# First group's outputs turned between the last graphs' products, with the first layer's tiles in a pool of their own

## The chip, the cores and the metric

One core of one Trainium2 chip runs the whole program in one launch. The metric is device time in microseconds (us) of one execution, lower is better. Times of several runs are compared by their median.

## The reference, cut to what matters

64 graphs of 256 nodes with 256 features go through two layers, both with a layer norm in front and a residual behind.

```python
# layer 0: graph convolution
h = relu(layernorm(x));  x = x + relu(norm(adj + I) @ h @ W.T + b)
# layer 1, on h = relu(layernorm(x)):
c = relu(bn1(conv1x1(h.T)))                  # conv1
x_conv = relu(bn2(conv17(c)) + h.T).T        # convolution of width 17 along the nodes
s = h @ w_se.T + b_se                        # 3 columns
A = exp(-squared_distance(s, s)) * adj
x_nmp = A @ relu(h @ w_msg.T + b_msg)        # message passing
x = x + GRU(input=[x_conv, x_nmp], state=h)  # gates r, z, n with w_ih, w_hh
```

## The kernel before, in words

**Stages.** Graphs come in four groups of 16 (`NG = 16`, `GROUPS = 4`). The first stage is the loop `for n in range(4, B + 5)` (B = 64): a pipeline over all graphs, in which one turn does one step for each of several graphs. Graph n is aggregated (`ag`) and projected (`o`), graph n-2 is turned (`ht`) and makes its messages (`ms`) and `conv1` (`c`), pairs of graphs get their distances (`st`, `di`, then `e` on ScalarE, `aT` on VectorE or GpSimd), and graph n-5 passes its messages (`nm`, evicted by ScalarE as `xnT` and stored to `xnd` in DRAM). For n of 66, 67 and 68 only the tail of this pipeline is left: the distances of graphs 62 and 63, `conv1` of 63, and the messages of graphs 61, 62 and 63. The second stage is the gates, the loop `for q in range(1, GROUPS + 1)`: 16 graphs in each turn.

**The convolution.** It is done group by group with a Fourier transform of 48 points over overlapping windows. For each graph two spectra (`df`) go from `h1l`, a load of what `conv1` stored, into the tile Xf; 24 steps of products (`y`) with the transformed filter follow; an inverse transform, written as a queue of small steps on VectorE, GpSimd and ScalarE, leaves the outputs in Xf and scr. This queue is `paced`: `beat(us)` is called between PE's pieces of work, runs what `after(k, ...)` has put down for k beats later, and issues as much of the queue as `share` allows; `paced.drain()` issues all that is left. The first group's convolution runs inside the first stage. Group q's outputs must then be turned by 64 PE transposes, four to a PSUM bank (16 banks, `yt`), and evicted with bias and relu into `xcT`, in turns by ScalarE and VectorE. `turn_outputs` does this at the head of each gate loop turn, ahead of the spectra of the next group.

**Order.** PE, VectorE, ScalarE, GpSimd and the DMAs put on `sp` are pinned to the program's order (class `Pinned`), so the order in which the kernel's lines run is the order on each engine. DMAs through `nc.sync` go on the same queue of SyncE (SP), at a place that the scheduler finds. The spectra load ahead by three graphs (`H1 = 3`): the load of graph g+3 is issued when the spectra of graph g are done.

**Memory.** The first stage's pools `ps` (5 PSUM banks), `ps_own` (3 banks), `wts`, `io`, `work` and `small` are closed together at the end of the first stage. The pools of the gates are opened behind that: `ps_m` (3 banks), `ps_gate` (5 banks), and `gates`, which holds xcT (32 KB a partition), the gate weights wiT and whT, and T1 to T4. These lie where the closed pools lay, so their first writers wait for the last users of the closed pools: the load of whT and, before the change, the first evictions into xcT wait for the last message product nm(63) and the last store from xnT. T1 to T4 are made from whT and wiT on GpSimd. The four products `first` write a value into the gates' PSUM banks, and ScalarE copies biases over it. The other state of the convolution (Xf, scr, the streams h1l, wf, xs) is in pools on the right side, which stay open.

**Names and lines.** In the profile almost all instructions carry line 102 (the helper that pins them), so tiles tell them apart. L293 is the load h1l, L328 wf, L1125 the store xnd, L1390 and L1391 the loads of whT and wiT, L1420 and L1421 the two halves of hx, L1427 h2l, L1431 x2l.

Of the kernel before, what the change touches and what calls it, by code (L numbers as in the profile page):

```python
# [11 lines left out]
FP = mybir.dt.float32  # L12
AF = mybir.ActivationFunctionType
ALU = mybir.AluOpType
# [14 lines left out]
OUT = 32  # L29
# [156 lines left out]
def gnn_kernel(  # L186
# [10 lines left out]
    B, N, D = x.shape  # L197
    P = 128
    KW = conv2_w.shape[2]
    NB = N // P  # L200
    DC = D // P
    G = 2
    NR = G * NB
# [25 lines left out]
    ident = const.tile([P, P], FP, tag="ident", name="ident")  # L229
# [15 lines left out]
    paced = Paced(pool, vec, act)  # L245

    def after(beats, go):
        due.append([beats, go])
# [274 lines left out]
                residual(k + 2)  # L523
                k += 1

    def turn_outputs(xcT):

        flip = 0
        for n0 in range(0, OUT, 4):
            for oc in range(DC):  # L530
                t = cv.bank(f"yt_{cv.q}_{n0}_{oc}").rearrange("p (i t) -> p i t", i=4)
                for i in range(4):
                    pe.transpose(
                        t[:, i, :], cv.y[n0 + i][:, oc * P : (oc + 1) * P], ident
                    )
                if (n0 // 4 * DC + oc) % 3 == 2:
                    cv.beat(1.3)
                dst, src = xcT[:, oc, :, n0 : n0 + 4], t.rearrange("p i t -> p t i")
                bias = sh[:, DC + oc : DC + oc + 1]
                flip ^= 1  # L540
                if flip:
                    act.activation(dst, src, AF.Relu, bias=bias)
                else:
                    vec.tensor_scalar(dst, src, bias, 0.0, ALU.add, ALU.max)


    with ExitStack() as one:
        ps = one.enter_context(tc.tile_pool(name="ps", bufs=5, space=PSUM))
        ps_own = one.enter_context(tc.tile_pool(name="ps_own", bufs=1, space=PSUM))
        wts = one.enter_context(tc.tile_pool(name="wts", bufs=1))  # L550
        io = one.enter_context(tc.tile_pool(name="io", bufs=2))
        work = one.enter_context(tc.tile_pool(name="work", bufs=2))
        small = one.enter_context(tc.tile_pool(name="small", bufs=3))
        taps_stack = ExitStack()
        taps = taps_stack.enter_context(tc.tile_pool(name="taps", bufs=1))

# [2 lines left out]
        def beat(us):  # L559
            come_due()  # L560
            paced.issue(*(k * us for k in share))
# [321 lines left out]
        def layer0_in(g, rows):  # L883

            xt, _ = st[g]["both"]
            rsd, nmr, dis = st[g]["rsd"], st[g]["nmr0"], st[g]["dis0"]
            if rows[0] == 0:
                hs = work.tile([P, NR, D], FP, tag="hs", name=f"hs_{g}")
                for b in range(G):
                    rb = slice(b * NB, (b + 1) * NB)  # L890
                    st[g + b].update(hs=hs[:, rb, :], dis=dis[:, rb])
            for r in rows:
                act.activation(
                    st[g + r // NB]["hs"][:, r % NB, :], xt[:, r, :], AF.Relu,
                    bias=nmr[:, r : r + 1], scale=rsd[:, r : r + 1],
                )

        def turn_adj(g, at=(1, 2), by=pool):
            s = st[g]
            t = bank(f"at_{g}").rearrange("p (c i) -> p c i", c=NB)  # L900
            for jc in range(NB):
                for ic in range(NB):
                    pe.transpose(
                        t[:, jc, ic * P : (ic + 1) * P], s["at"][:, ic, jc * P : (jc + 1) * P], ident
                    )

            def keep():
                s["adjT"] = work.tile([P, NB, N], FP, tag="adjT", name=f"adjT_{g}", bufs=6)
                act.copy(s["adjT"], t)

            def hat():
                s["adjH"] = work.tile([P, NB, N], FP, tag="adjH", name=f"adjH_{g}")
                by.tensor_tensor(s["adjH"], s["adjT"], eye, ALU.add)
            after(at[0], keep)
            if at[1] is None:
                return hat
            after(at[1], hat)

        def aggregate(g):
            s = st[g]  # L920
            t = bank(f"ag_{g}").rearrange("p (c i) -> p c i", c=DC)
            for fc in range(DC):
                for jc in range(NB):
                    pe.matmul(
                        t[:, fc, :], s["hs"][:, jc, fc * P : (fc + 1) * P], s["adjH"][:, jc, :],
                        start=(jc == 0), stop=(jc == NB - 1),
                    )

            def keep():
                s["aggT"] = work.tile([P, DC, N], FP, tag="aggT", name=f"aggT_{g}")  # L930
                act.copy(s["aggT"], t)
            after(1, keep)

# [314 lines left out]
        def item(filter_too=False):  # L1248
            if filtering and not filter_too:
                return  # L1250
            pace[1] = min(pace[1] + pace[0], 1.0)
            if items and pace[1] > 0.999:
                pace[1] -= 1.0
                items.pop(0)()
# [29 lines left out]
        begin()  # L1284
        for n in range(4, B + 5):
            even, odd = n % G == 0, n % G == 1
            if filtering and not items:
                filtering.clear()
                while due:
                    beat(0.0)  # L1290
                conv_start()
            if n == B - 2:

                share[:] = 0.45, 0.6, 0.33
            elif n == B:
                share[:] = 0.65, 0.75, 0.4
            if even and n + 2 * G < B:
                load(n + 2 * G)
            if n <= B + 1:
                turn_h(n - 2)  # L1300
            beat(0.4)
            item()
            if n < B:
                aggregate(n)
                if odd and n + 1 < B:
                    after(2, lambda n=n: factors(n + 1))
                    for r in range(NR):
                        after((5, 7, 8, 9)[r], lambda r=r, n=n: layer0_in(n + 1, (r,)))
                if even and n < B - G:
                    for r in (0, 2):  # L1310
                        after(1 + r // 2, lambda r=r, n=n: row_moments(n + G, (r, r + 1)))
                if even and n + G < B:
                    after(4, lambda n=n: degrees(n + G))
            beat(1.7)
            item()
            if even and n <= B + 2:
                turn_cols(n - 4)
            beat(0.2)
            if n + 1 < B:
                turn_adj(n + 1)  # L1320
            beat(0.4)
            item()
            if n >= 5:
                pass_messages(n - 5)
            beat(1.7)
            item(True)
            if n <= B + 1:
                messages(n - 2)
            beat(1.7)
            item()  # L1330
            if even and n <= B + 2:
                distance(n - 4)
            beat(0.6)
            item()
            if n < B:
                project(n)
            beat(1.7)
            item(True)
            if n <= B:
                conv1(n - 2)  # L1340
            elif n == B + 2:
                conv1(B - 1)
            beat(1.7)
            item()
            if later:
                for go in later.pop(0):
                    go()
                if not later:
                    while due:
                        beat(0.0)  # L1350
                    prep_stack.close()
                    spec_stack = ExitStack()
                    spec = spec_stack.enter_context(tc.tile_pool(name="spec", bufs=1))
                    tab = spec.tile([P, 3 * UNITS], FP, tag="tab", name="tab")
                    nc.sync.dma_start(tab, nc.inline_tensor(filter_table(), name="tab_c").ap())
                    tp = {k: filter_load(k) for k in range(2)}
                    filtering.append(True)
                    pace[:] = FILTER / 2, -7.0
                    items.extend(
                        lambda k=k, j=j: filter_part(k, j) for k in range(4) for j in range(QC // 8)  # L1360
                    )
        while items:
            item()
        for g in range(H1):
            h1_load(1, g)
        while due:
# [14 lines left out]
    cv.beat = beat  # L1381
    cv.bank = lambda name: ps_m.tile([P, 2 * D], FP, tag="m", name=name)

    def outputs_turned(q):
        return big.tile([P, DC, P, OUT], FP, tag="xcT", name=f"xcT_{q}")

    xcT = outputs_turned(1)
    wiT = big.tile([P, 2 * DC, 3 * D], FP, tag="wiT", name="wiT")
    whT = big.tile([P, DC, 3 * D], FP, tag="whT", name="whT")
    nc.sync.dma_start(whT, wh_d)  # L1390
# [220 lines left out]
    for q in range(1, GROUPS + 1):  # L1611
# [1 line left out]
        ld = gate_inputs(q - 1, 0)  # L1613
        paced.drain()
        if q > 1:
            xcT = outputs_turned(q)
        turn_outputs(xcT)
        for go in gate_parts(ld, xcT):
            go()
        todo = []  # L1620
# [57 lines left out]
```

## Time and profile before

| | us |
|---|---|
| median of 3 runs (2075.66, 2078.24, 2078.29) | 2078.24 |
| the profiled execution | 2076.19 |
| its span, first to last instruction | 2074.4 |
| PE busy in it (98%) | 2029.9 |
| DVE, ACT, POOL busy | 1403.6, 999.2, 1108.7 |
| mean granted PE clock | 0.997 |

A line of a timeline gives the start, the length from the first start to the last end, the engine, the line, the operation with out<-in, the count, and in brackets how long the engine was idle before it and what ended that. The program's fp32 matmuls run as two passes, so `nm` of one graph shows as x8; a transpose is one. SPq lines are the issue of a DMA and not its transfer. A windows line gives for each engine the busy time in that stretch, then the granted clock of PE, the mean share of the DMA engines that was busy, and GB/s.

### The profile page before, as it was taken

The page shows a single profiled execution, that of the slowest core. Times are in us where ns is not written, and L with a number is a line of the kernel's source. Part 1 is how long each engine was busy: PE and PEld are TensorE (multiplying, and loading weights), DVE is VectorE, ACT ScalarE, POOL GpSimd, SP SyncE. Part 2 cuts the span into 40 slices and gives each one's busy share as a digit, 9 for nine tenths or more (in the row PEclk, how much of TensorE's full clock was granted, in tenths as well). Part 3 has the DMA queues.
Part 4 walks back from the last instruction along what each step waited for, and adds up shares of the span by engine and source line. Part 5 has one row for each costly group of instructions (what it writes and reads, how often), then busy time and mean ns, then how long its engine had stood idle before and what let it go on. Part 6 is the DMA issues. An engine that isn't in the chain of part 4 may idle for free. (4 is left out here: it accounts for less than half of the span.)

```text
span 2074.4 us, 31212 instructions
## 1 busy us (share of the span) xinstructions
PE 2029.9 (98%) x9977; PEld 1728.6 (83%) x9977; DVE 1403.6 (68%) x3172; ACT 999.2 (48%) x2171; POOL 1108.7 (53%) x1326
## 2 busy tenths in 40 slices
PE   7999999999999999999999999999999999999998
PEld 6877777888888787788888888888888888888887
DVE  5656666544688888237889815989924989965444
ACT  5756666665457676522344532234442234443333
POOL 4343333334775665347667527766626767644433
PEclk9999999999999999999999999999999999999999
DMA  8797987656765554656333455533446524322331
GB/s 282 261 259 245 265 257 248 208 178 224 240 206 198 178 178 138 212 178 204 122 117 117 137 176 190 168 101 118 124 152 199 155 92 129 116 87 89 95 96 61
DMA packets 292488, 352.84 MB, mean 170 GB/s; under 512 B 19523, under 2 KB 232150, under 8 KB 291670
## 3 DMA queue, kind: packets, MB, share of 16 engines
q1 hardware_dynamic: 292038, 346.40, 53.1%
q0 software_dynamic: 288, 4.46, 0.6%
q8 instruction: 80, 1.31, 0.3%
q14 instruction: 82, 0.67, 0.1%
HBM read 224.43 MB, written 126.35 MB: 169 GB/s over the span
## 5 line engine op out<-in xcount | busy, mean ns | idle before, releaser
L102 DVE TENSOR_TENSOR Xf<-y,k 128x256 f32<-128x256 f32 x184 | 69.0, 416 | 177.8 <-PE y L102 174.8
L102 DVE SCALAR_TENSOR_TENSOR Xf<-Xf 128x256 f32<-128x256 f32 (+1 forms) x248 | 185.1, 760 | 6.2 <-ACT Xf L102 5.1
L102 PE MATMUL ta<-T,S 128*128 128x256 f32 x768 | 186.6, 379 | 0.0
L102 PE MATMUL y<-wf,Xf 128*128 128x256 f32 x768 | 182.5, 380 | 1.8 <-DVE Xf L102 1.4
L102 POOL TENSOR_TENSOR rz<-u,p 128x256 f32<-128x256 f32 x64 | 47.8, 747 | 244.4 <-ACT u L102 244.4
L102 POOL TENSOR_TENSOR rs<-ve,mhalf 128x2 f32<-128x2 f32 x65 | 52.1, 801 | 220.0 <-DVE nm L102 218.7
L102 ACT ACTIVATE rz<-rz 128x512 f32<-128x512 f32 x128 | 80.3, 627 | 180.8 <-DVE rz L102 180.8
L102 PEld LDWEIGHTS y<-wf,Xf 128*128 128x128 f32 x768 | 143.9, 190 | 24.1 <-DVE Xf L102 2.6
L102 PEld LDWEIGHTS ta<-T,S 128*128 128x128 f32 x768 | 145.9, 190 | 19.8
L102 PE MATMUL n<-wiT,hx 128*128 128x256 f32 x512 | 152.3, 379 | 0.0
L102 POOL TENSOR_TENSOR xs<-Xf 128x256 f32<-128x256 f32 x92 | 69.8, 765 | 136.2 <-PE y L102 72.2
L102 DVE SCALAR_TENSOR_TENSOR h2l<-rz,h2l 128x256 f32<-128x256 f32 x128 | 102.9, 804 | 53.4 <-POOL h2l L102 53.4
L102 POOL TENSOR_TENSOR aT<-e,adjT 128x512 f32<-128x512 f32 x62 | 83.1, 1357 | 95.0 <-ACT e L102 95.0
L102 PE MATMUL ms<-wmT,h2T 128*128 128x259 f32 x512 | 127.2, 391 | 4.4 <-ACT h2T L102 4.4
L102 PE MATMUL n<-whT,hx 128*128 128x256 f32 x512 | 131.4, 379 | 0.0
L102 PE MATMUL n<-wiT,xcT 128*128 128x256 f32 x512 | 131.4, 379 | 0.0
L102 PE MATMUL nm<-aT,mso 128*128 128x256 f32 x512 | 123.3, 385 | 6.1 <-DVE pre L102 3.6
L102 PE MATMUL ag<-adjH,hs 128*128 128x256 f32 x512 | 124.3, 385 | 4.8 <-POOL adjH L102 2.7
L102 POOL TENSOR_TENSOR adjH<-adjT,eye 128x512 f32<-128x512 f32 x63 | 82.2, 1305 | 83.0 <-ACT adjT L102 81.2
L102 PE MATMUL o<-w0T,aggT 128*128 128x256 f32 x512 | 124.0, 385 | 1.4 <-ACT e L102 0.9
L102 PEld LDWEIGHTS ms<-wmT,h2T 128*128 128x128 f32 x512 | 97.8, 194 | 32.1 <-issue 12.9
L102 PE MATMUL c<-w1T,h2T 128*128 128x256 f32 x512 | 123.0, 383 | 0.0
(190 smaller groups left out, 5259.4 us busy)
## 6 DMA issues: line engine op xcount, KB each, us to landing
wf<-wfd SPq DMA_DIRECT2D x284, 256.0 KB
wfd<-fo SPq DMA_DIRECT2D x32, 576.0 KB
x2d<-x SPq DMA_DIRECT2D x64, 256.0 KB
h2d<-h SPq DMA_DIRECT2D x64, 256.0 KB
hTd<-h2T SPq DMA_DIRECT2D x64, 256.0 KB
h1d<-c1o SPq DMA_DIRECT2D x64, 256.0 KB
xnd<-xnT SPq DMA_DIRECT2D x64, 256.0 KB
h1l<-h1d SPq DMA_DIRECT2D x64, 256.0 KB
```

The source lines that it names most:

```text
L102: return self.tc.keep_in_program_order(getattr(self.engine, op)(*args, **kwargs))
```

## The change

Three things are done.

- `hs`, `adjH` and `aggT`, tiles of the first layer, move from pool `work` to pool `io`, with the same two buffers. `io` (with x and adj, too) gets a stack of its own, `front_stack`, opened behind `small`.
- At n = B + 2 = 66 `front_stack` is closed, a pool `turned` for xcT is opened on the right side, and the paced queue is drained. xcT of all groups comes from this pool, and no longer from `gates`.
- `turn_outputs` is split: `turn_part_of` writes the four transposes of one bank and hands back its eviction. The first group's 16 banks are placed in the last turns of the first stage: one at n = 66 behind the messages of graph 61, three at the end of n = 66, six at n = 67 ahead of the messages of graph 62, and two times three behind the loop. Each eviction is put down for the next beat. They use the first stage's `bank` (5 PSUM buffers). For groups two to four the same banks are turned at the head of the gate loop, as before.

```diff
-    def turn_outputs(xcT):
-
-        flip = 0
-        for n0 in range(0, OUT, 4):
-            for oc in range(DC):
-                t = cv.bank(f"yt_{cv.q}_{n0}_{oc}").rearrange("p (i t) -> p i t", i=4)
...
+    def outputs_turned():
+        return cv.turned.tile([P, DC, P, OUT], FP, tag="xcT", name=f"xcT_{cv.q + 1}")
+
+    def turn_part_of(xcT, k):
+
+        n0, oc = k // DC * 4, k % DC
+        t = cv.bank(f"yt_{cv.q}_{n0}_{oc}").rearrange("p (i t) -> p i t", i=4)
+        for i in range(4):
+            pe.transpose(t[:, i, :], cv.y[n0 + i][:, oc * P : (oc + 1) * P], ident)
+        dst, src = xcT[:, oc, :, n0 : n0 + 4], t.rearrange("p i t -> p t i")
+        bias = sh[:, DC + oc : DC + oc + 1]
+
+        def keep():
+            if k % 2 == 0:
+                act.activation(dst, src, AF.Relu, bias=bias)
+            else:
+                vec.tensor_scalar(dst, src, bias, 0.0, ALU.add, ALU.max)
+        return keep
+
+    TURNS = OUT // 4 * DC
+
+    def turn_outputs(xcT, ks=range(TURNS)):
+        for k in ks:
+            keep = turn_part_of(xcT, k)
+            if k % 3 == 2:
+                cv.beat(1.3)
+            keep()
...
-        io = one.enter_context(tc.tile_pool(name="io", bufs=2))
         work = one.enter_context(tc.tile_pool(name="work", bufs=2))
         small = one.enter_context(tc.tile_pool(name="small", bufs=3))
+
+        front_stack = ExitStack()
+        io = front_stack.enter_context(tc.tile_pool(name="io", bufs=2))
...
-                hs = work.tile([P, NR, D], FP, tag="hs", name=f"hs_{g}")
+                hs = io.tile([P, NR, D], FP, tag="hs", name=f"hs_{g}")
...
         for n in range(4, B + 5):
             even, odd = n % G == 0, n % G == 1
+            if n == B + 2:
+
+                front_stack.close()
+                cv.turned = ctx.enter_context(tc.tile_pool(name="turned", bufs=1, side="right"))
+                paced.drain()
+                xcT, parts_left = outputs_turned(), list(range(TURNS))
+
+                def turns(m):
+                    for _ in range(m):
+                        after(0, turn_part_of(xcT, parts_left.pop(0)))
...
+            if n == B + 3:
+                turns(6)
+                beat(0.0)
             if n >= 5:
                 pass_messages(n - 5)
             beat(1.7)
+            if n == B + 2:
+                turns(1)
             item(True)
...
             elif n == B + 2:
                 conv1(B - 1)
             beat(1.7)
+            if n == B + 2:
+                turns(3)
+                beat(0.0)
             item()
...
         while items:
             item()
+        for _ in range(2):
+            turns(3)
+            beat(0.0)
         for g in range(H1):
             h1_load(1, g)
...
-    def outputs_turned(q):
-        return big.tile([P, DC, P, OUT], FP, tag="xcT", name=f"xcT_{q}")
-
-    xcT = outputs_turned(1)
...
         if q > 1:
-            xcT = outputs_turned(q)
-        turn_outputs(xcT)
+            xcT = outputs_turned()
+            turn_outputs(xcT)
```

More of the change, by code (lines that the diff above doesn't have):

```diff
@@ L524, in inverse_last @@
                 k += 1
-    def turn_outputs(xcT):
-        flip = 0
-        for n0 in range(0, OUT, 4):
-            for oc in range(DC):
-                t = cv.bank(f"yt_{cv.q}_{n0}_{oc}").rearrange("p (i t) -> p i t", i=4)
[L532 to L544, printed above, removed]
+    def outputs_turned():
[20 more added lines that the diff above has]
+            keep()
     with ExitStack() as one:
@@ L911, in hat @@
             def hat():
-                s["adjH"] = work.tile([P, NB, N], FP, tag="adjH", name=f"adjH_{g}")
+                s["adjH"] = io.tile([P, NB, N], FP, tag="adjH", name=f"adjH_{g}")
                 by.tensor_tensor(s["adjH"], s["adjT"], eye, ALU.add)
@@ L929, in keep @@
             def keep():
-                s["aggT"] = work.tile([P, DC, N], FP, tag="aggT", name=f"aggT_{g}")
+                s["aggT"] = io.tile([P, DC, N], FP, tag="aggT", name=f"aggT_{g}")
                 act.copy(s["aggT"], t)
```

## The prediction

> **What bounds the kernel now.** I read the busy table first: PE is busy for 2029.9 of 2074.4 us (98%), so only time in which PE idles or runs at a lower clock can be won. The chain that ended last shows only the final two DVE instructions and says nothing of the middle. So I cut the span into windows of 20 us: from 840 to 860 us PE is busy for 17.59 us only. That is the seam between the first layer and the gates, the place of the change. There I went through the timelines engine by engine. PE first; the columns are start, length, instruction, and the idle time before it with what ended it.
>
> ```profile
> 834.64 1.89 PE L102 MATMUL nm<-aT,mso 128*128 128x256 f32 x8
> 836.46 0.71 PE L102 MATMUL di<-R,L 5*128 5x256 f32 x8
> 837.11 1.99 PE L102 MATMUL c<-w1T,h2T 128*128 128x256 f32 x8
> 838.93 3.62 PE L102 MATMUL nm<-aT,mso 128*128 128x256 f32 x16
> 843.27 1.14 PE L102 MATMUL first<-brzB,ident 32*128 32x512 f32 x8 [0.72 <-ACT xnT L102]
> ...
> 846.82 1.94 PE L102 MATMUL yt<-ident,Xf 128*128 128x128 f32 x14 [0.94 <-ACT xcT L102]
> ...
> 853.20 5.13 PE L102 MATMUL df<-dft,h1l 128*128 128x240 f32 x24
> 859.07 5.48 PE L102 MATMUL df<-dft,h1l 128*128 128x240 f32 x24 [0.75 <-DMA h1l<-h1d]
> 864.85 16.44 PE L102 MATMUL df<-dft,h1l 128*128 128x240 f32 x80 [0.29 <-DMA h1l<-h1d]
> 881.12 4.02 PE L102 MATMUL y<-wf,Xf 128*128 128x256 f32 x16
> ```
>
> To be seen: after the last message product (end 842.55) come `first`, the 64 transposes `yt` (844.34 to 853.20) and the spectra `df`, and the spectra already wait for loads. Then the same stretch on SP, which issues the DMAs in program order:
>
> ```profile
> 841.52 2.05 SPq L1125 DMA_DIRECT2D xnd<-xnT  x2
> 845.43 0.32 SPq L1390 DMA_DIRECT2D whT<-whd  x1
> 845.80 0.42 SPq L1391 DMA_DIRECT2D wiT<-wid  x1
> 846.27 0.43 SPq L1420 DMA_DIRECT2D hx<-hTd  x1
> 846.74 0.85 SPq L1421 DMA_DIRECT2D hx<-xnd  x1
> ...
> 855.11 0.32 SPq L293 DMA_DIRECT2D h1l<-h1d  x1
> ```
>
> The gates' weights whT (768 KB) and wiT (1536 KB) go out only when the last `xnd` store has landed, 2.88 us after the last message product, and the fourth `h1l` (256 KB) stands behind them. Last, windows of 1 us after a PE gap of 2.53 us (the third number from the right is the granted clock):
>
> ```profile
> 826.00:827.00 1.00, 0.00 (x0) 0.00 (x0) 1.00 (x4) 1.00 (x5) 0.00 (x0) 1.00 0.00 0
> ...
> 829.00:830.00 1.00, 1.00 (x4) 0.82 (x3) 0.90 (x3) 0.75 (x3) 0.58 (x1) 0.50 0.14 38
> 830.00:831.00 1.00, 1.00 (x3) 0.73 (x3) 1.00 (x2) 0.18 (x1) 1.00 (x2) 0.50 0.91 257
> ```
>
> An idle PE comes back at half clock. The four rows from 828 to 832 have 0.68, 0.50, 0.50, 0.61: 1.71 us lost. The gap of 2.1 us at 143 us cost about the same (0.85, 0.50, 0.50, 0.50, 0.95).
>
> **The change, part by part.** It adds and removes no instruction: the built orders show the same instructions, and apart from the seam the same sequence, on all engines (groups two to four turn their outputs as before).
>
> *The pools.* hs, adjH and aggT keep their two buffers, only at another address; before the seam no wait changes. Cost 0; I see no row that would price an address. The paced work of the first group ends on DVE at 833.3 and on POOL at 833.9, ahead of the point where it is now drained: cost 0, bounds 0 to 0.4 us (one 128x256 DVE operation ahead of the column copies).
>
> *The wait that goes.* Before, xcT lies over the closed pools, so its first writes wait for the same `xnd` store as whT (landed by 845.43; DVE's first eviction starts at 845.63, ACT's at 846.09 behind its bias copies), and PE stands 0.94 us. That goes. The other 52 of the 64 transposes then take 6.38 us, 0.49 us a bank of four, with three banks; bare transposes follow each other in 0.11 us, 0.44 a bank. With five banks, and evictions of 0.69 us (ACT) and 0.75 us (DVE) taking turns, the evictions need 0.75 us per two banks, less than PE, and no longer bind. I take 0.46 a bank, bounds 0.44 and 0.53.
>
> *The new order on PE.* One bank after nm(61), nine between c(63) and nm(62), six after nm(63). The ten banks ahead of nm(63) make its end 842.55 + 10 x 0.46 = 847.15. What they wait for is there: aT(62) follows e, which slips by one ACT eviction (0.69) to about 839.2, and nm(62) stands at 843.5. Six banks: 849.9. `first` now has to wait until the last bank is evicted (its latency 0.17, DVE 0.75, a semaphore 0.06: 1.0) : 850.9; `first` takes 1.07 (843.27 to 844.34): the spectra start at 851.95 instead of 853.20. **Gain on PE 1.25 us.** The idle of 2.53 us at 825 and its half clock lie ahead of the seam and stay.
>
> *What is moved with it.* nm(63) ends 4.6 us later, so the last `xnd` store, and whT, wiT, hx behind it on SP, go out 4.6 us later: whT at 850.03. Behind nm(63) on ACT stands only its own copy, so nothing is added there. POOL's T products wait for wiT; they ended at 862 and would end at 866.6, and the first gate needs them at 891: hidden by the spectra. But the fourth `h1l` is late. The new order on SP helps it: hx of the second graph and h2l now stand behind it. Ahead of it remain whT, wiT and two hx, 2.88 MB, with itself 3.15 MB. By the 1 us windows the queue before had moved 3.15 MB at 854.6, 9.2 us after the issue of whT (no bytes in the first 1.3 us). What waits sees its data later than that: T on POOL 0.9 us (wiT, 853.56), S on DVE 2.4 us (hx, 856.36), PE 1.7 us (3.93 MB by 857.3, spectra at 859.07). I take 1.7, the row of the same tile: 850.03 + 9.2 + 1.7 = **860.9**, bounds 860.1 and 861.6 (with 0.53 a bank 862.3). The spectra ask for it at 851.95 + 6 x 0.81 = 856.8. PE stands 4.1 us, where before it stood 1.0 (858.06 to 859.07).
>
> *After the stall.* Before, the remaining 26 spectra took 22.05 us (859.07 to 881.12) where 26 x 0.81 = 21.06 would do; 1.0 us was waiting for the next loads. In the new order the fifth and sixth `h1l` land right behind the fourth, and the seventh (4.72 MB, moved by 15.1 us after whT's issue, 866.8 with the lag) is asked for at 860.9 + 4.86 + 1.7 = 867.5: I take that wait as 0, bound 1.0. The half clock I take at 1.7, bounds 0 and 1.8: the gap is longer than the two gaps that cost that much. So the products start at 860.9 + 21.06 + 1.7 = 883.7 instead of 881.12: **+2.6 us**. From there PE is nearly always busy (1207.6 of 1220 us from 840 to 2060) and nothing later absorbs a shift. 2076.19 + 2.6 = **2078.8 us** (span 2074.4 + 2.6, and the 1.8 us around it). The profiled execution lies 2.05 us under the median shown, 2078.24; against that it would be 2080.8.
>
> *Two rules against it.* The Trainium skill, TensorE: Matmul & The Clock Gate, Part 1, sets the clock down after an idle window of about 3.4 us. The gaps of 2.1 and 2.5 us above contradict that as a limit for one gap; if it held strictly and the stall were just under 3.4, the sum would be +0.9 us. The Trainium skill, DMA: Bandwidth & Descriptors, Specifications, gives 435 GB/s as the ceiling: estimate 3.15 MB in 7.2 us, `h1l` there at about 858.6, a short stall, products at 879.6, 1.5 us earlier than before. The rows have 3.15 MB in 7.9 us and a lag behind it.
>
> **The rivals.**
> - *The load is not late* (it lands as wiT did, or the scheduler's earlier place on SP is worth more than I count). Then 851.95 + 32 x 0.81 = 877.9, 3.2 us early: 2073.0. For it: the first three `h1l` are there long before. Against: DMA is full (0.96 to 1.10) from 847 to 852 already.
> - *Late, but no half clock*: 860.9 + 21.06 = 882.0, +0.9: 2077.1. For it: gaps of 0.7 to 1.1 us had none. Against: three longer gaps had it.
> - *Slower by more than 0.2%*: the load block starves the spectra further. With 0.53 a bank and the lag of hx (2.4), the fourth `h1l` is there at 850.7 + 9.2 + 2.4 = 862.3; with 1.75 of half clock and a second wait of 1.0 at the seventh: 886.1, +5.0: 2081.2. It decides from a start of the fourth graph's spectra at 862.5 on, or 861.5 with the second wait. For it: before, DMA is at 0.74 to 1.10 from 847 to 863, and now 4.6 us later. Against: hx and h2l have moved behind.
> - *It gains more than 0.2%*: the first rival's 3.2 us, 0.3 from 0.44 a bank, and 0.5 if the last bank is evicted in half the time, make 4.0: 2072.2, not even then. It would take something that I do not see.
>
> That the turns do not move is excluded by the built order.
>
> **How the numbers follow.** 0.2% is 4.2 us, about what a measurement of this kernel can tell from no change. Forecast (late, half clock) 0.55; late without half clock 0.15; not late 0.13; further starved 0.14; a gain over 4.2 us 0.03. The first three lie within 0.2%: 0.83. The range runs from the first rival, 2073.5, to the starved case with the 2 us by which runs differ, 2083.0.
>
> **What would show it.** Right: nm(63) ends near 847; whT goes out near 850; PE waits some 4 us for `h1l` after six spectra (24 `df` rows), with clock rows of 0.5 behind; xcT's evictions wait for `yt` alone; products near 883.7. Wrong: spectra without a wait (first rival), no rows of 0.5, a second wait at the seventh graph, or evictions that stop `yt` between the products. Any difference ahead of 834 us would be a cost of the pools that I put at 0.

## The result, and the profile after

The changed kernel takes 2080.6 us (median of 20 runs, 2078.38 to 2084.06), the kernel before 2077.62 us in 20 runs beside it: ratio 1.0018, 95% interval 1.0012 to 1.0024, so 2.98 us slower by the medians. The profiled execution takes 2079.66 us (span 2077.9); predicted were 2078.8 against a profiled 2076.19, and 2080.8 against the median.

The PE timeline of the changed kernel through the seam, in the columns of the prediction's first fence:

```profile
833.86 0.66 PE L102 MATMUL st<-ident,cols 128*128 128x128 f32 x4 [2.74 <-DVE cols L102]
...
843.30 3.62 PE L102 MATMUL nm<-aT,mso 128*128 128x256 f32 x16
846.76 2.13 PE L102 MATMUL yt<-ident,Xf 128*128 128x128 f32 x18
...
850.48 1.14 PE L102 MATMUL first<-brzB,ident 32*128 32x512 f32 x8 [0.93 <-DVE xcT L102]
851.55 5.13 PE L102 MATMUL df<-dft,h1l 128*128 128x240 f32 x24
859.89 10.02 PE L102 MATMUL df<-dft,h1l 128*128 128x240 f32 x40 [3.22 <-DMA h1l<-h1d]
870.65 13.20 PE L102 MATMUL df<-dft,h1l 128*128 128x240 f32 x64 [0.74 <-DMA h1l<-h1d]
883.69 4.02 PE L102 MATMUL y<-wf,Xf 128*128 128x256 f32 x16
```

The transposes now lie ahead of the second `nm` row and behind it; PE goes from them into `first` and the spectra `df`, which start 1.65 us earlier than before (851.55 against 853.20; 0.28 us of that lies ahead of the seam). Then PE stands 3.22 us for the fourth `h1l`, where it stood 0.75 us, and 0.74 us again at the ninth. SP's timeline of the same kernel shows why the load is late:

```profile
845.89 2.04 SPq L1135 DMA_DIRECT2D xnd<-xnT  x2
849.79 0.32 SPq L1417 DMA_DIRECT2D whT<-whd  x1
850.16 0.42 SPq L1418 DMA_DIRECT2D wiT<-wid  x1
...
853.46 3.56 SPq L293 DMA_DIRECT2D h1l<-h1d  x3
```

whT goes out at 849.79 instead of 845.43, since the last `xnd` store comes behind ten more banks of transposes. The fourth `h1l` goes out at 853.46, when the first graph's spectra have freed a buffer, and 6.43 us later PE goes on. The windows of 1 us of PE around the stall (busy share, granted clock, DMA share, GB/s):

```profile
857.00:858.00 1.00, 0.00 (x0) 1.00 0.96 367
858.00:859.00 1.00, 0.00 (x0) 1.00 1.05 406
...
860.00:861.00 1.00, 1.00 (x4) 0.70 0.90 307
861.00:862.00 1.00, 1.00 (x4) 0.50 1.02 387
862.00:863.00 1.00, 1.00 (x4) 0.50 0.70 252
863.00:864.00 1.00, 1.00 (x4) 0.59 0.24 43
```

PE idles while the DMA engines are full, and comes back at half clock: 0.30 + 0.50 + 0.50 + 0.41 = 1.71 us lost. The span grew by 3.5 us: -0.28 ahead of the seam (start of `st`), +2.85 in it (`st` to the first products `y`: 46.98 before, 49.83 now), +0.93 behind it.

### The profile page after: what moved, and what is told of

Same layout as the page of the kernel before. It is cut to its first block, busy times and chain, and to the rows that moved or that the text cites. A ratio compares the mean times of both kernels' runs of the same rounds, so it can differ in the third digit from the quotient of the medians.

```text
span 2077.9 us, 31212 instructions
## 1 busy us (share of the span) xinstructions
PE 2028.0 (98%) x9977; PEld 1727.6 (83%) x9977; DVE 1402.2 (67%) x3172; ACT 998.8 (48%) x2171; POOL 1108.9 (53%) x1326
```

## The experiments

Executions reach the seam at different times, so I compare inside it. In the table, "stall" is PE's wait for the fourth `h1l`, with later ones of the same tile behind a plus, and "half" the time lost to half clock inside the seam. All are from the one profiled execution of each kernel, while the ratio to the kernel before is from the timed runs.

| kernel | st to spectra | stall | half | st to products | ratio (95%) |
|---|---|---|---|---|---|
| before | 19.06 | 0.75 + 0.29 | 0 | 46.98 | 1 |
| changed | 17.69 | 3.22 + 0.74 | 1.7 | 49.83 | 1.0018 (1.0012 to 1.0024) |
| pools_only | 19.05 | 0.67 + 0.16 | 0 | 46.38 | 0.9999 (0.9990 to 1.0008) |
| first_last | 19.66 | 1.08 | 0 | 47.00 | 1.0002 (0.9993 to 1.0010) |
| pools_first_last | 19.69 | 1.57 | 1.5, at `st` | 47.52 | 0.9997 (0.9987 to 1.0006) |
| behind | 17.40 | 1.97 | 1.7 | 47.32 | 1.0001 (0.9992 to 1.0010) |
| behind_wi_twice | 17.40 | 4.98 | 2.0 | 50.85 | 1.0020 (1.0011 to 1.0029) |
| extra | 17.69 | 0 + 0.76 | 0 | 44.72 | 0.9988 (0.9979 to 0.9997) |
| behind_extra | 17.40 | 0 | 0 | 43.43 | 0.9989 (0.9980 to 0.9998) |
| act_queue | 17.69 | 3.23 | 1.6 | 48.78 | 1.0002 (0.9993 to 1.0012) |
| early_wh_pin | 17.69 | 1.63 | 0 | 45.58 | 0.9989 (0.9981 to 0.9998) |
| before_pin2 | 19.05 | 0 | 0 | 45.07 | 0.9995 (0.9986 to 1.0004) |
| behind_pin2 | 17.40 | 0.26 | 0 | 43.92 | 0.9984 (0.9976 to 0.9993) |

**Theory:** the seam is longer because whT and wiT go out later and the spectra's fourth load stands behind them. **Rivals:** the pools' new addresses cost the time (A); the turns between the products cost PE time (C); the DMA's bandwidth binds anyway, so that a stall only moves (D).

### One part at a time: pools_only, behind

pools_only is the changed kernel with the turns put back to the head of the gates:

```diff
-            if n == B + 2:
-                turns(1)
...
         if q > 1:
             xcT = outputs_turned()
-            turn_outputs(xcT)
+        turn_outputs(xcT)
```

> Only the pools and the drain of the change; the turns stand where they stood before, with three PSUM buffers. Theory (the later loads cost the time): the first xcT eviction no longer waits for the last xnd store, so the spectra start 0.9 to 1.1 us earlier than before (852.1 to 852.3 in the profile), but whT goes out as early as before (845 to 846), so the fourth h1l still lands at 858.5 to 859.2: the gain turns into a longer wait of PE for h1l (1.5 to 2.2 us instead of 0.75), the products start at 881 (880.6 to 881.6), or at 882.5 if the clock halves behind that wait; ratio 0.9995 to 1.001. Rival A (the pools' new addresses cost the time): products as late as in the changed kernel, 883 to 884, or a loss ahead of 834 us; ratio 1.0015 to 1.002. Rival B (the removed wait is a gain in full): products at 880, ratio 0.9995.

The ratio and the products are those of the theory (46.38 from `st`, the fourth `h1l` 13.57 us after whT's issue, against 13.64 before), and rival A is out as the cause of the loss: with the new addresses the kernel is no slower than before, to within 0.1%. (Behind the products its traced execution takes 1.27 us longer than that of before, 1194.55 against 1193.28 us; pools_first_last, with the same pools, has 1193.31.) One expectation missed: the spectra did not start earlier. PE waited as long as before the change, though no closed pool lies under xcT any more. The PE row and ACT's rows of pools_only, then ACT's rows of before:

```profile
847.84 1.94 PE L102 MATMUL yt<-ident,Xf 128*128 128x128 f32 x14 [0.95 <-ACT xcT L102]
```

```profile
845.45 0.38 ACT L102 COPY ta<-brzB 128x256 f32<-128x256 f32 x1 [1.21 <-PE first L102]
845.76 0.37 ACT L102 COPY tc<-brzB 128x256 f32<-128x256 f32 x1
846.07 1.10 ACT L102 COPY n<-bnB 128x512 f32<-128x512 f32 x2
847.11 1.26 ACT L102 ACTIVATE xcT<-yt,sh 128x512 f32<-128x512 f32 x2
```

```profile
845.05 1.10 ACT L102 COPY n<-bnB 128x512 f32<-128x512 f32 x2
846.09 1.25 ACT L102 ACTIVATE xcT<-yt,sh 128x512 f32<-128x512 f32 x2
```

In both, ACT's first eviction stands without a gap behind its four bias copies for `first` (ta, tc and two of n). In pools_only these, not the store, end the wait. The next section but one takes that apart.

behind keeps five PSUM buffers and turns all banks behind the last `nm`:

```diff
...
-        for _ in range(2):
-            turns(3)
+        for m in (3, 3, 3, 3, 3, 1):
+            turns(m)
             beat(0.0)
```

> The change with all 16 banks turned behind the last message product, still in five PSUM buffers, none between the products. Theory (the later loads cost the time): the last xnd store and whT go out some 4.4 us earlier than in the changed kernel (whT at 845 to 846), PE has the same work ahead of the spectra, so these start where they start in the changed kernel, 851.3 to 852; the fourth h1l lands at 858.5 to 859.2, so PE waits 1.7 to 2.8 us; products at 881 without, at 882.5 with a stretch of half clock; 1 to 2.7 us less than the changed kernel, ratio to before 0.999 to 1.0007. Rival A (the pools' addresses cost the time): as slow as the changed kernel, ratio 1.0015 to 1.002. Rival C (turns between the products cost PE time of their own, loads do not matter): the spectra start more than 1 us earlier than in the changed kernel, 850.5 or before, and the wait for h1l stays as long as in the changed kernel, 3.2 us.

PE of behind:

```profile
858.46 22.98 PE L102 MATMUL df<-dft,h1l 128*128 128x240 f32 x104 [1.97 <-DMA h1l<-h1d]
```

As the theory has it: whT at 845.24, spectra at 851.36, stall 1.97 us, products at 881.28, 2.51 us less from `st` than the changed kernel. Of these, 1.25 us are the shorter stall, 0.74 the second wait that is gone, 0.29 the earlier spectra, and 0.23 is in none of these rows (a wait in brackets counts from the modelled end of the last matmul and so falls short of the delay of the next start: 0.74 for some 0.9 us at the second wait). The 0.29 us is all that is left of rival C. Against before, the wait that went came back as a stall and half clock: ratio 1.0001.

### The stall alone: extra, behind_extra, early_wh_pin, behind_wi_twice

extra is the changed kernel with the fourth to sixth `h1l` loaded at n = 66 into tiles of their own; behind_extra the same on behind:

```diff
...
+                cv.more = ctx.enter_context(tc.tile_pool(name="more", bufs=1, side="right"))
+                for g in range(H1, 2 * H1):
+                    h1 = cv.more.tile([P, NB, D], FP, tag=f"h1m{g}", name=f"h1m_{g}")
+                    nc.sync.dma_start(h1, h1_d[NG + g].rearrange("p (c d) -> p c d", c=NB))
+                    cv.h1[1, g] = h1
```

> The change as it is, turns between the products, but the fourth to sixth h1l of the second group are loaded ahead of the seam into tiles of their own, so that six graphs of spectra wait for nothing behind whT and wiT. Theory: whT still goes out near 850, the spectra start near 851.6, and PE does not stand at the fourth graph; no rows of half clock there; products at 877.5 to 878.5 (a wait of up to 1 us at the seventh graph is possible), 5 to 6 us less than the changed kernel and 2.7 to 3.6 less than before; ratio to before 0.998 to 0.9988. Rival A or C (addresses, or the order of the turns on PE): the time stays that of the changed kernel, ratio 1.0015 to 1.002, whatever the spectra wait for. Rival D (the stall only moves to later graphs, bandwidth binds): PE waits 2 to 3 us at the seventh graph instead, products at 881 to 883.

> The turns behind the last message product as in the run named behind, and the three extra h1l tiles. Theory: with the loads ahead neither place of the turns starves the spectra, so this one and the run named extra come out alike: spectra at 851.3 to 852, products at 877.5 to 878.5, ratio to before 0.998 to 0.9988, within 0.5 us of each other at the products. Rival C (the place of the turns itself counts): this one is 1 us or more ahead of the run named extra at the products. Rival D (bandwidth binds): a wait of 2 to 3 us at the seventh graph in the run named extra, less here.

PE of extra:

```profile
857.25 5.02 PE L102 MATMUL df<-dft,h1m 128*128 128x240 f32 x24
862.11 5.02 PE L102 MATMUL df<-dft,h1l 128*128 128x240 f32 x24
867.90 11.58 PE L102 MATMUL df<-dft,h1l 128*128 128x240 f32 x56 [0.76 <-DMA h1l<-h1d]
879.32 4.02 PE L102 MATMUL y<-wf,Xf 128*128 128x256 f32 x16
```

With the turns between the products and whT as late as in the change (850.57), taking the stall away takes 5.11 us off the seam: 3.22 of stall, 1.7 of half clock. Rival D shows in small (0.76 us at the tenth graph's load, not 2 to 3). The two kernels differ by 1.29 us at the products in the profile, more than I expected, and that is the mark I had set for rival C. But only 0.29 of it is the spectra's start; 0.76, as counted in the brackets, is that wait for a load. Their ratios cannot be told apart.

early_wh_pin takes whT out of the way (in the new pool, loaded ahead of the seam). Up to the fourth `h1l` the rest of the order is the change's; behind it, all `h1l` go ahead of the loads of later graphs, by the edit described below for before_pin2, so that only its first wait is to be compared:

```diff
+                cv.whT = cv.turned.tile([P, DC, 3 * D], FP, tag="whT", name="whT")
+                nc.sync.dma_start(cv.whT, wh_d)
...
-    nc.sync.dma_start(whT, wh_d)
+    whT = cv.whT
     nc.sync.dma_start(wiT, wi_d)
...
```

> The change as it is, turns between the products, but whT (0.79 MB) has a tile in the new pool and is loaded ahead of the seam; the loads keep the change's order up to the fourth h1l, with 2.36 MB up to and with it instead of 3.15. Theory (the bytes asked for from the seam on set the stall, 0.39 MB per us): 2.0 us less, PE waits 0.9 to 1.6 us for the fourth h1l instead of 3.22, and no half clock follows, since PE does not idle for 1.8 us within one window; from st to the products 45 to 46.5 us instead of 49.83; ratio to before 0.9990 to 0.9999. Rival (the stall is the latency from the issue of the load itself, or what the turns do): the wait stays 3 us, with half clock behind it, 49 us or more, ratio 1.001 to 1.002.

The stall fell by 1.59 us to 1.63, just past the end of what I expected (1.6), and no half clock followed:

```profile
859.16 21.30 PE L102 MATMUL df<-dft,h1l 128*128 128x240 f32 x104 [1.63 <-DMA h1l<-h1d]
```

From the issue of the first of the weights to PE's go on it takes 8.43 us instead of 10.10: 0.79 MB for 1.67 us. behind_wi_twice goes the other way, with wiT loaded twice on behind (no more than a repeated load):

```diff
     nc.sync.dma_start(wiT, wi_d)
+    nc.sync.dma_start(wiT, wi_d)
```

> The run named behind, with wiT loaded twice (the same data into the same tile); the second load and three of hx stand ahead of the fourth h1l: 4.98 MB up to and with it instead of 3.93. Theory (the queue's bytes ahead of the fourth h1l set the stall): 1.05 MB more at 0.39 MB per us is 2.7 us more: PE waits 4.3 to 5.2 us instead of 1.97; from st to the products 50 us (49.3 to 51) instead of 47.32; ratio to before 1.0008 to 1.0020. Rival (the stall is not set by these bytes): the wait stays 2 us, st to the products 47.3, ratio as for behind, 1.000.

Stall 4.98, `st` to products 50.85, ratio 1.0020. The size does not prove the rate, though: the second load had to wait for the first to land (issued at 853.94), and the fourth `h1l` behind it went out only at 854.30.

### What the removed wait was for: first_last, pools_first_last

first_last leaves the pools of before and moves the products `first`, with ACT's copies behind them, from ahead of the transposes to behind them; pools_first_last does that on pools_only.

```diff
-    for r, tag in enumerate(("ta", "tc", "n", "n")):
...
         turn_outputs(xcT)
+        if q == 1:
+            for r, tag in enumerate(("ta", "tc", "n", "n")):
...
```

> The kernel before, its pools and three PSUM buffers unchanged; only the four small products called first (and with them ACT's bias copies, which wait for them) stand behind the 64 transposes instead of ahead of them. It tells what the 0.94 us wait of PE was for. Theory Q (ACT's queue: the bias copies of 1.66 us stood ahead of ACT's first eviction): the first evictions start 0.3 us after the first transposes, at 843 to 844, ahead of the time at which whT goes out (845.2 to 845.8); PE stands less than 0.4 us in a stretch between the transposes; from the start of the last column transposes st to the spectra 18.0 to 18.4 us instead of 19.06. Theory S (my prediction's: xcT lies over closed pools and waits for the last xnd store): no eviction before 845.2; PE stands 1.5 to 2.2 us after three banks; st to spectra 19.6 to 20.2 us. In both the fourth h1l lands where it did, 858.5 to 859.2, so the products start within 0.7 us of before (plus 1.7 if the clock halves); ratio 0.9995 to 1.001.

> Both edits of the runs named pools_only and first_last together: xcT in the pool of its own, and first with ACT's bias copies behind the transposes; turns at the head of the gates as before, three PSUM buffers, loads in the order of pools_only. Theory Q and S together (two waits of nearly one length lay over each other, so that either alone leaves PE standing 0.95 or 1.48 us): no stretch of PE's waiting for xcT is longer than 0.35 us, and from st to the spectra it takes 18.0 to 18.5 us instead of 19.05 and 19.66. Theory B (three PSUM buffers are what holds PE, whatever the evictions wait for): 0.9 us or more of waiting stays, st to the spectra 18.9 or more. The fourth h1l lands at the same time after whT's issue as in pools_only (13.6 us), so st to the products stays within 46 to 47.2 us (1.7 more with half clock); ratio 0.999 to 1.001.

In first_last the store does hold the evictions, as theory S has it. The PE and the ACT row:

```profile
847.01 1.94 PE L102 MATMUL yt<-ident,Xf 128*128 128x128 f32 x14 [1.48 <-ACT xcT L102]
```

```profile
846.27 1.27 ACT L102 ACTIVATE xcT<-yt,sh 128x512 f32<-128x512 f32 x2 [2.32 <-DMA xnd<-xnT]
```

With both edits (pools_first_last) no wait for xcT is left at all; the row in which it stood has no idle time ahead of it:

```profile
845.47 2.50 PE L102 MATMUL yt<-ident,Xf 128*128 128x128 f32 x18
```

From `st` the spectra start after 19.69 us, not 18.0 to 18.5, because this execution ran `st` and the first `nm` behind it at half clock (1.54 us lost ahead of the transposes). Counted from the second-last message product, which starts behind that stretch, the four kernels need 14.27 (before), 14.26 (pools_only), 14.87 (first_last) and 13.36 us (both). So two waits of about the same length lay over each other, and either alone kept PE standing. Three PSUM buffers are not the limit (theory B): the 13.36 us were made with them. Less the 1.54 us, `st` to products is 45.98, at the lower end of what was expected.

### Whose bytes: act_queue

```diff
-        nc.sync.dma_start(h1, h1_d[q * NG + g]
+        (act if q == 1 and g >= H1 else nc.sync).dma_start(h1, h1_d[q * NG + g]
```

> The change as it is, with the thirteen h1l issued on ACT's queue instead of SP's; the same bytes are in flight. It tells whether the fourth h1l is late because it stands behind whT, wiT and hx in one queue, or because the bandwidth is used up. Theory ring: a queue of its own shares the DMA engines with SP's, so the fourth h1l lands 2 us or more earlier after its issue, PE waits 0 to 1.2 us instead of 3.22, no half clock, st to the products 44.7 to 46.5 us instead of 49.83; ratio to before 0.9985 to 0.9998. Theory bandwidth: the bytes asked for first are moved first whatever the queue; PE still waits 2.7 to 3.5 us; st to the products 49 to 50.3; ratio 1.001 to 1.002. ACT has each issue between its copies of the spectra; if they delay these, PE waits for ACT in many small steps.

The fourth `h1l` was issued at 853.21 and let PE go at 859.64, 6.43 us later; in the changed kernel 853.46 and 859.89, 6.43 us too. A queue of its own did not help this load. In the trace's DMA records its packets start at 856.6, 3.4 us after the issue, and from 857 to 861 the two queues move 0.40 MB per us, 0.23 on SP's and 0.17 on ACT's; so neither theory holds as I put it. The second wait went (0.74 us). The ratio, 1.0002, came out lower than the 1.001 I expected; a seam 1.80 us longer than before's would make 1.0009, which lies within its interval.

### The order alone: before_pin2, behind_pin2

Both issue the thirteen `h1l` ahead of hx, h2l and x2l of the later graphs, by putting these loads on SP in program order (`sp.dma_start` in place of `nc.sync.dma_start`); before_pin2 does nothing else to the kernel before.

> The run named behind with the same loads, but issued on SP in the order whT, wiT, two hx of the first graph, and then all thirteen h1l ahead of hx, h2l and x2l of the later graphs. Theory: 3.15 MB up to the fourth h1l instead of 3.93, 2.0 us less: it is there at about 856.4 when the spectra ask for it at 856.2: PE waits 0 to 0.6 us, no half clock there; from st to the products 43.5 to 44.5 us instead of 47.32; ratio to before 0.9983 to 0.9993. Rival D (the bytes are only moved, and hx or wf come too late for the gates): products as early, but PE waits 2 us or more for hx, h2l or wf between 885 and 930, ratio 0.9995 to 1.001. Rival A (something else than the loads makes the seam long): st to the products stays above 46.

> The kernel before with no part of the change, only the loads in the order of the run named behind_pin2 (the thirteen h1l ahead of hx, h2l and x2l of the later graphs). It tells how much of that run's gain is the order of the loads alone. Theory: the spectra start 19.06 us after st as before, the fourth h1l is there before they ask for it, so from st to the products 19.06 + 32 x 0.81 = 45.0 to 45.4 us instead of 46.98: 1.6 to 2.0 us less than before, and 1.1 to 1.5 us more than behind_pin2 (43.92), which is what the earlier spectra of the change are worth once the loads do not hide it; ratio to before 0.9988 to 0.9996. Rival (the order gives all of the gain, the place of the turns nothing): st to the products 43.9, ratio 0.998 to 0.9988. Rival (order alone gives nothing): 46.9, ratio 1.000.

PE of behind_pin2, then of before_pin2 (a row without brackets has no wait ahead of it):

```profile
858.28 21.30 PE L102 MATMUL df<-dft,h1l 128*128 128x240 f32 x104 [0.26 <-DMA h1l<-h1d]
879.41 4.02 PE L102 MATMUL y<-wf,Xf 128*128 128x256 f32 x16
```

```profile
853.09 26.19 PE L102 MATMUL df<-dft,h1l 128*128 128x240 f32 x128
879.11 4.02 PE L102 MATMUL y<-wf,Xf 128*128 128x256 f32 x16
```

Both seams are as the theory has them. The order alone takes 1.91 us off the seam of before (ratio not to be told from 1), and with the loads out of the way the change's earlier spectra are worth another 1.15 us. behind_pin2 has the lowest ratio of the study, though its interval overlaps with those of extra, behind_extra, early_wh_pin and before_pin2: 2074.21 us against 2078.05, ratio 0.9984 (0.9976 to 0.9993). Its last 0.26 us is a wait for the fourth `h1l`: issued at 854.80, when the first graph's spectra free its buffer, it lets PE go on 3.48 us later. This is not the least that the load takes: in before_pin2 it was issued at 855.01 and held nothing up at 858.05, 3.04 us later. There the DMA engines had run nearly dry (49 and 6 GB/s from 854 to 856), while in behind_pin2 they were still moving 354 and 162 GB/s; that these bytes make the difference is likely, but no run shows it.

## Why the prediction was right

- **Bound and place** (PE at 98%, the seam): right. pools_only shows no cost of the pools that its interval of 0.1% could tell. The idle of 2.53 us at 825 stayed; its half clock did not in the traced execution, which won nothing by it, since PE then waited 2.74 us for `cols` at `st` instead of 1.06.
- **The wait that goes: right in size, wrong in cause.** The prediction has the evictions wait for the `xnd` store. The store landed by 845.43, but ACT's first eviction, which held PE, started at 846.09 right behind its bias copies. Its row was before me, and I set the copies down as a remark. The two lay over each other, and by the runs with `first` moved the wait goes only because the change also puts `first` behind the turns.
- **The new order on PE**: gain 1.37 us (19.06 to 17.69), forecast 1.25. A bank took 0.436 us, not 0.46; nm(63) ended at 846.92, forecast 847.15; the wait ahead of `first` was 0.93, forecast 1.0.
- **What is moved with it: right, and the step that decided.** whT at 849.79 (850.03), the fourth `h1l` at 859.89 (860.9), stall 3.22 (4.1). The windows have 3.15 MB moved at 858.9, 9.1 us after whT's issue (9.2). The lag behind the bytes is the term mis-sized: 1.0 us, where the prediction took 1.7 from the row of before. extra, behind and early_wh_pin show that this stall and what follows it is the loss.
- **After the stall**: half clock 1.7, as forecast. The second wait, taken as 0 with a bound of 1.0 at the seventh graph, was 0.74 at the ninth. It offset the shorter stall, so that the products at 883.69, forecast 883.7, agree to a hundredth by luck; from `st` it is 49.83 us against 49.6.
- **"Nothing later absorbs a shift"**: the shift was not absorbed, but 0.93 us came on top behind the products. PE's waits for the filter stream `wf` are 0.9 us there (one of 0.40 at 917.26), and before has none of them; but its waits for `h1l` are 0.3 us shorter, and all its idle time from the first products to the last matmul grew by 0.45 us (9.55 to 10.00), half of the 0.93. Between the kernels this last part of the span varies from 1192.8 to 1194.6 us, and not in step with the seam: pools_only has 1194.55. What sets it stays open.
- **The sum**: forecast +2.6 us; by the medians it is 2.98, between the two profiled executions 3.47. The range's lower end, 2073.5, is put down to the first rival, whose own sum is 2073.0.
- **Rivals**: "not late" and "starved further" did not come; "no half clock" did not in this execution. The Trainium skill's ceiling of 435 GB/s (DMA: Bandwidth & Descriptors, Specifications) held for the bytes in flight: 442, 455, 418 and 418 GB/s in the windows from 852 to 856, 433 in the mean. But the load was no earlier for it, since the queue's first 2 us moved little (61 GB/s from 850 to 851) and the data was seen 1.0 us behind its last byte.

## What to carry to other kernels

When work is moved ahead of a product or a store that releases other things, count what hangs on that release. Here, turning in the first stage starts the spectra 1.4 to 1.7 us earlier, but the ten banks ahead of the last `nm` add nothing to that (17.69 against 17.40 us) and send 2.4 MB of loads out 4.4 us later, ahead of loads that PE needs sooner. Before a wait is written off as removed, look at what else ends at the same time: a wait goes only when the second-last cause goes too, as the runs with `first` moved show. The remedy was cheap: what is needed first goes first into the queue.

## What the runs showed of the hardware

**The half clock follows a fixed grid.** The traces hold records of the granted clock. By those of the thirteen traces, half clock comes in stretches of 3.413 us, and within one execution they start a whole number of such stretches apart (9, 30, 200, 240); the grid lies elsewhere in each execution. Summing PE's idle time by grid stretch behind the first 20 us: all 33 stretches with 2.08 us or more of idle were followed by one at half clock; of those with 1.50 to 1.78 us none was, except around 41 us, where a stretch that already ran at half clock was followed by another after 0.90 to 1.49 us of idle. Between 1.86 and 1.99 us two were and four were not. So a gap costs by where it falls: the 2.53 us ahead of the seam lies within one stretch before the change and is followed by half clock, and in the traced execution of the changed kernel lies across two and is not. By these bounds a stall of 3.22 us has half clock behind it wherever it leaves 2.1 us in one stretch, one of 1.97 (behind) had it in the traced execution, and one of 1.63 (early_wh_pin) should not have it unless other idle time falls into the same stretch. The 1.7 us of the changed kernel are so in part a matter of the execution: a stall of 3.22 us that lies across two stretches with less than 2.08 us in each may have none, which is at most 0.94 us of the 3.41 in which it can start (an estimate from these figures). The Trainium skill, TensorE: Matmul & The Clock Gate, Part 1, tells of a free-running window of this length, which agrees; that it takes a whole idle window to lose the clock does not: some 60% of one was enough.
